# Eight transfers of each image issued from ScalarE's queue instead of SP's, with a lag margin in the planner

## The chip, the core and the metric

The kernel runs on one core of a Trainium2 chip. A core has five engines that run beside each other, each through its own list of instructions in order: TensorE (PE, matrix products), VectorE (DVE), ScalarE (ACT), GpSimd (POOL) and SyncE (SP), which in this kernel only issues DMA transfers. The metric is the device time of one execution in microseconds (us), the median of several runs.

## The reference

The input is x of shape (32, 96, 56, 56). Two layers follow. Each adds its result to x and begins with g, which is x normalised to mean 0 and variance 1 over groups of three channels with their planes (`gn`, with 1e-5 added to the variance); the kernel takes the statistics in `group_stats`.

Layer 0 is an inverted bottleneck with 4-bit weights and activations and a residual:

```python
g = gn(x)
h = act_q(bn(conv1x1(g, quant_w(w1)), ...))      # 96 -> 576
h = act_q(bn(depthwise3x3(h, quant_w(w2)), ...)) # 576, one 3x3 filter per channel
x = x + (g + bn(conv1x1(h, quant_w(w3)), ...))   # 576 -> 96
```

Layer 1 splits the channels of g = gn(x) into three parts of 32 (x_0, x_05, x_1) and adds a convolution of their results to x:

```python
x_0  = group_conv3x3(x_0, conv0_w * gate)                         # spatial part
Fre  = frft2d(x_05, alpha); Mix = group_conv1x1([Fre.real, Fre.imag], ...)
x_05 = abs(frft2d(Mix, -alpha)) / (H * W)                         # fractional part
x_1  = irfft2(group_conv1x1(rfft2(x_1) as real and imaginary))    # Fourier part
x    = x + conv3x3(concat(x_0, x_05, x_1), conv2_w) + conv2_b
```

alpha, the order of the fractional Fourier transform, comes for each image from a small network on the means of its own channels.

## The kernel before, in words

Images are handled one after another, but three streams are interleaved: the head of layer 0 (load, statistics, split), its body, and layer 1 of an earlier image. While layer 1 of image i runs, the body of layer 0 of image i+1 fills the gaps. Here and below the short names are those of the tiles in the profile.

*Layer 0.* `load` (L474) brings x. `split` (L704 to L710) normalises it and writes it as a high part hi (ScalarE) and the remainder lo (GpSimd). `expand` (L717) multiplies by w1 into the PSUM tile pe, in blocks b of 128 channels and four pixel parities u; ScalarE turns pe into 4-bit levels q1s (L662) and VectorE makes them integers (L666). `leave` and `enter` (L738, L746) bring q1s through DRAM (sd) into the layout d in which `depthwise` (L756) can run on TensorE, into pd. The same follows with q2s, gd and q (L777, L780), and `project` (L786) multiplies q by w3 into pp, which VectorE adds to x (L796). Names such as pe_0_3 and pd_0 are block and parity, and the group counted through.

*Layer 1.* After the statistics (L643, L651) `norm` (L863) writes the normalised middle 32 channels into rows 64 to 95 of F. `leave_x` stores them to DRAM (xd, L868), and `enter_x` loads them in two halves with image rows on the partitions (xh, L875). `forward_h` (pf, L975), `forward_w` (pu, L986), `inverse_w` (pi, L1002) and `inverse_h` (pv, L1013) are the transforms; their result pq is stored to DRAM (`leave_pq`: pd, L1024) and loaded back into F with channels on the partitions, in four transfers (`enter_pq`: L1029 twice and L1033 twice). `mix_f` (pz, L1047) multiplies F by the gated weights; squares, a square root and copies to the tile cat follow (L1054 to L1060). The spatial part writes ps (L1126) and the Fourier part pt, pr and px (L1069 to L1112); ScalarE and VectorE copy them to cat too (L1140, L1118, L1120). From cat VectorE forms the Winograd tiles V (L1158 to L1167) and TensorE the final convolution pc (L1179). `hidden`, `gate_row` and `gates` (ph, pg, pa, po) make the gates and alpha's table tab; outer (L907) and tab (L964) are ScalarE's part of it. The DRAM tile pd of the fractional part and the PSUM tile pd of the depthwise share a name.

*Buffers.* pe, pd (PSUM) and pp share two pairs of PSUM banks ("pair"); ps, px, pz, pc and the others of layer 1 share four single banks ("bank"). A matmul that takes a buffer again waits until the engine that reads it is through.

*The order.* `arrange` first writes the steps of the streams in a program order by estimated costs. Then `Order` computes the dependencies of all instructions, models a duration and a lag for each (`model`), packs them by list scheduling forward and backward in several trials (`pack`, `schedule`), and fixes the best trial's order on every engine (`hold`). So each engine's order is decided when the program is built. For a DMA the lag is the time from issue to data: 1.6 us, the time for its bytes, and 0.3 more for some. `moved` in `pack` is a running end of all transfers issued so far: one total for the whole core, so that in the plan a transfer stands behind all earlier ones.

Before the change every transfer of the main part is issued on SP, in one list. An SP instruction that waits (for VectorE, for an earlier transfer) holds all behind it. ScalarE issues only the constants at the start.

Of the kernel before, what the change touches and what calls it, by code (L numbers as in the profile page):

```python
# [63 lines left out]
C, H, W = 96, 56, 56  # L64
# [10 lines left out]
G = 32  # L75
# [3 lines left out]
BN_EPS = 1e-5  # L79
WINDOW, CHANGE = 3.4133, 0.09  # L80
TURNS, NEAR = 8, (2.0, 4.0, 8.0)
SLACK = 0.3


# [58 lines left out]
class Order:  # L143
# [64 lines left out]
    def model(self):  # L208


        self.took, self.lag, self.port, self.move, self.kind, self.work = [], [], [], [], [], []
        for i, e, access in zip(self.ins, self.eng, self.access):
            outs, ins = [a for a, w in access if w], [a for a, w in access if not w]
            n = max([_count(a) for a, _ in access], default=1)
            psum = [self.tiles.get(a.tensor.name, "")[:2] == "ps" for a in ins]
            wide = [a for a in ins if _count(a) > 1]
            lag = {"PE": 0.2, "Pool": 0.08}.get(e, 0.04)
            port, move, kind, work = False, 0.0, None, 0.0
            if i.opcode == "DMACopy":
                took = 0.47 if e == "SP" else 0.4  # L220
                for a in (outs[0], ins[0]):
                    run = size = _bytes(a.dtype)
                    dims, n = list(a.ap), 1.0
                    if self.tiles.get(a.tensor.name, "dram") != "dram":
                        n = dims.pop(0)[1]
                        move = max(move, _count(a) * size / 7000.0 * min(n / 16.0, 1.0))
                    for _, c in dims:
                        n *= c
                    for step, c in reversed(dims):
                        if step * size == run or c == 1:  # L230
                            run *= c
                        else:
                            break
                    run = min(run, n * size / 16)
                    move = max(move, math.ceil(n * size / run / 16) * (0.011 + run / 21e3))
                lag = 1.6 + move + (0.3 if ins[0].tensor.name.startswith(("in_x", "sd", "gd")) else 0.0)
            elif e == "PE":
                cols, weights, rows = _count(ins[0]), _count(ins[1]), ins[0].ap[0][1]
                full = all(str(a.dtype) == "dt.float32" for a in ins)
                beside = weights in (G, 64) and cols >= HN  # L240
                if i.is_transpose:
                    took = max(cols / 1175.0, 0.055)
                    work = cols / 1200.0
                elif full:
                    took = 2 * max(cols / 1175.0, min(weights * 0.85e-3, 1.0), 0.05)
                    work = cols / 600.0
                else:
                    took = max(cols / (2180.0 if "float32r" in str(ins[1].dtype) else 2350.0), 0.05)
                    work = cols / 2400.0
                if beside and not i.is_transpose:  # L250
                    took, work = took * weights / 128.0, work * weights / 128.0
                kind = (0 if rows <= 32 else 1 if rows <= 64 else 2), weights if beside else 0
                work *= rows / 128.0
            elif e == "Activation":
                out = _count(outs[0])
                bias = sum(_count(a) == 1 for a in ins) > 1
                took = 0.1 + bias * 0.1 + out / 960.0 + (0.08 if out > 700 and psum[0] else 0.13 if out < 8 else 0.0)
            elif e == "DVE":
                port = n > 8 and not any(psum)
                if port and i.opcode == "TensorScalarPtr" and len(wide) == 1:  # L260
                    took = 0.15 + n / 1920.0 + (0.12 if n >= 700 else 0.0)
                else:
                    port = port and len(wide) > 1
                    took = (0.14 if n > 8 else 0.16) + n / 960.0 + (0.06 if any(psum) and "ScalarPtr" in i.opcode else 0.0)
            elif e == "Pool":
                port = True
                took = 0.1 + n * (2.25 if len(wide) > 1 else 1.1) / 1000.0 if n > 8 else 0.5
            else:
                took = 0.1
            self.took.append(took)  # L270
            self.lag.append(lag)
            self.port.append(port)
            self.move.append(move)
            self.kind.append(kind)
            self.work.append(work)

    def pack(self, before, rank, near=0.0, back=False):
# [3 lines left out]
        n = len(self.ins)  # L281
# [4 lines left out]
        engines = sorted(set(self.eng))  # L286
        free, held = dict.fromkeys(engines, 0.0), dict.fromkeys(("DVE", "Pool"), 0.0)
        soon, now = {e: [] for e in engines}, {e: [] for e in engines}
        start, end, kind, moved = [0.0] * n, [0.0] * n, None, 0.0
        window, much, fast = 0, 0.0, False  # L290
        for k in range(n):
            if not lacks[k]:
# [1 line left out]
        for _ in range(n):  # L294
            t, e = min((free[e] if now[e] else max(free[e], soon[e][0][0]), e) for e in engines if now[e] or soon[e])
            while soon[e] and soon[e][0][0] <= t:
                k = heapq.heappop(soon[e])[1]
                heapq.heappush(now[e], (rank[k], k))
            k = now[e][0][1]
            if e == "PE" and near and self.kind[k] != kind:  # L300
                k = min([x for x in now[e] if self.kind[x[1]] == kind and x[0] < rank[k] + near], default=now[e][0])[1]
            if k == now[e][0][1]:
                heapq.heappop(now[e])
            else:
                now[e].remove((rank[k], k))
                heapq.heapify(now[e])
            if self.port[k]:
                t = max(t, held["Pool" if e == "DVE" else "DVE"])
            took = self.took[k]
            start[k], end[k] = t, t + took  # L310
            if e == "PE" and not back:
                took += CHANGE if kind != self.kind[k] else 0.0
                kind = self.kind[k]
                x, left = t, took
                while left > 1e-9:
                    while x >= (window + 1) * WINDOW - 1e-9:
                        window, fast, much = window + 1, much > 0.365 * WINDOW, 0.0
                    pace = 1.0 if fast else 0.5
                    part = min(left, ((window + 1) * WINDOW - x) * pace)
                    much += self.work[k] * part / took  # L320
                    left, x = left - part, x + part / pace
                end[k] = x
            free[e] = end[k]
            if self.port[k]:
                held[e] = end[k]
            lag = self.lag[k]
            if self.move[k] and not back:
                moved = max(moved, end[k] + 0.63) + self.move[k]
                lag = moved + self.lag[k] - self.move[k] - 0.63 - end[k]
            for q in then[k]:  # L330
                first = q if back else k
                alike = self.eng[q] == e and self.ins[first].opcode != "DMACopy"
                ready[q] = max(ready[q], end[k] + (0.0 if alike else self.lag[q] if back else lag))
                lacks[q] -= 1
                if not lacks[q]:
                    heapq.heappush(soon[self.eng[q]], (ready[q], q))
# [111 lines left out]
def block_kernel(ctx: ExitStack, tc: tile.TileContext, out: bass.AP, a: dict):  # L448
    nc = tc.nc
# [404 lines left out]
    def layer1(i):  # L854
# [10 lines left out]
            )  # L865
        def leave_x():
            s["xd"] = dp.tile([G, HW], F32, tag="xd", name=f"xd{i}")
            nc.sync.dma_start(out=s["xd"], in_=s["F"][2 * G : 3 * G])  # L868

        def enter_x():  # L870

            s["xh"] = p1.tile([2 * H, G // 2, W], F32, tag="h", name=f"xh{i}")
            for q in range(2):
                src = s["xd"][G // 2 * q : G // 2 * (q + 1)].rearrange("c (h w) -> h c w", w=W)
                nc.sync.dma_start(out=s["xh"][H * q : H * (q + 1)], in_=src)  # L875

        def norm1():

# [142 lines left out]

        def leave_pq():
            s["pd"] = dp.tile([2 * H, G + 1, W], F32, tag="pd", name=f"pd{i}")
            nc.sync.dma_start(out=s["pd"], in_=s["pq"])  # L1024

        def enter_pq():
            for q in range(2):
                src = s["pd"][H * q : H * (q + 1)]
                nc.sync.dma_start(  # L1029
                    out=s["F"][G * q : G * (q + 1)].rearrange("c (h w) -> c h w", w=W),  # L1030
                    in_=src[:, :G, :].rearrange("h c w -> c h w"),
                )
                nc.sync.dma_start(  # L1033
                    out=s["F"][3 * G + q : 3 * G + q + 1].rearrange("c (h w) -> c h w", w=W),
                    in_=src[:, G : G + 1, :].rearrange("h c w -> c h w"),
                )
# [483 lines left out]
```

## Time and profile before

| | |
|---|---|
| median of three runs | 3358.4 us (3348.12 to 3361.56) |
| the profiled execution | 3364.8 us, of which its span on the core 3363.0 us |
| mean granted TensorE clock | 0.949 |
| DMA | 469.92 MB, 140 GB/s over the span |
| SP's ring of queues (q1) | 432384 packets, 51.6% of 16 engines' span |
| ScalarE's ring of queues (q10) | 4184 packets, 0.3% |

The profile is of one execution and its times are to be set against 3364.8 us. For each group of instructions it gives the line, the engine, what is written from what, how many there were, and the idle time of the engine just before them with what ended it. A float32 matmul counts twice, since it runs as two passes. The durations of DMA issues are the time the issuing engine was held, not that of the data. Of the transfers concerned the trace shows the following on SP, by their instructions' durations (lowest, median, highest):

| transfer | line | issues | us |
|---|---|---|---|
| xd<-F | L868 | 32 | 0.308, 0.320, 0.326 |
| xh<-xd | L875 | 64 | 0.395, 0.935, 1.778 |
| pd<-pq | L1024 | 32 | 0.319, 0.322, 0.416 |
| F<-pd, 32 rows | L1029 | 64 | 0.315, 0.658, 1.002 |
| F<-pd, 1 row | L1033 | 64 | 0.730, 1.984, 3.050 |

### The profile page before, as it was taken

What the parts mean: (1) busy time and instruction counts of PE and PEld (TensorE: products, weight loads), DVE (VectorE), ACT (ScalarE), POOL (GpSimd) and SP (SyncE); (2) the same over time, 40 slices, a digit from 0 to 9 for tenths busy, and PEclk for the clock granted to TensorE, in tenths of its full rate; (3) what the DMA queues carried; (4) which work ended last, traced back from release to release, by engine and by line L of the source; (5) the groups of instructions that cost most, each with busy time, mean ns of one, the idle gap of its engine ahead of it and who ended that gap; (6) DMA issues with size and microseconds to landing.
All of it is one profiled execution on the core that took longest, in us unless ns stands there. A gap on an engine that the chain in (4) does not pass through costs nothing. (4 is left out here: it accounts for less than half of the span.)

```text
span 3363.0 us, 47042 instructions
## 1 busy us (share of the span) xinstructions
PE 2961.3 (88%) x17024; PEld 1824.1 (54%) x17024; DVE 2331.5 (69%) x4497; ACT 2085.9 (62%) x2792; POOL 585.2 (17%) x657
## 2 busy tenths in 40 slices
PE   3789998889998889999899999898998898999987
PEld 2455565455565555555455565455565455565544
DVE  5357677677777676777677777676777676777755
ACT  3566665576666566656566666566666576666543
POOL 3122101222101222111222011222111222101100
PEclk9898999999999999999999999999999999999987
DMA  4545564455655455654455655455655455655432
GB/s 125 150 118 143 147 166 133 116 144 144 167 159 141 117 145 137 168 141 134 124 146 151 173 146 149 121 146 138 168 157 142 116 145 143 166 162 148 115 89 51
DMA packets 436800, 469.92 MB, mean 140 GB/s; under 512 B 203174, under 2 KB 351640, under 8 KB 435544
## 3 DMA queue, kind: packets, MB, share of 16 engines
q1 hardware_dynamic: 432384, 464.18, 51.6%
q10 hardware_dynamic: 4184, 2.74, 0.3%
q8 instruction: 135, 2.21, 0.3%
q14 instruction: 97, 0.79, 0.1%
HBM read 266.85 MB, written 199.97 MB: 139 GB/s over the span
## 5 line engine op out<-in xcount | busy, mean ns | idle before, releaser
L662 ACT ACTIVATE q2s<-pd,o,s 128x784 uint8<-128x784 f32 x576 | 558.3, 1002 | 473.9 <-PE pd L756 454.5
L1179 PE MATMUL pc<-V,wcw 96*96 96x392 f32 x2304 | 834.9, 502 | 18.1 <-DVE V L1164 18.1
L662 ACT ACTIVATE q1s<-pe,o,s 128x784 uint8<-128x784 f32 (+1 forms) x640 | 624.1, 1004 | 219.7 <-PE pe L717 213.5
L717 PE MATMUL pe<-hi,w1r 96*128 96x392 f32 x1280 | 532.7, 416 | 68.0 <-ACT q1s L662 32.1
L1179 PEld LDWEIGHTS pc<-V,wcw 96*96 96x96 f32 x2304 | 366.9, 164 | 338.9 <-issue 319.7
L756 PE MATMUL pd<-d,dw 128*64 128x392 fp8e4 x4608 | 471.1, 345 | 85.1 <-DMA d<-sd 78.2
L717 PE MATMUL pe<-lo,w1r 96*128 96x392 f32 x1280 | 440.6, 344 | 3.2 <-POOL lo L708 3.2
L756 PEld LDWEIGHTS <-dw 128*64 128x64 bf16 x4608 | 243.3, 113 | 297.8 <-DMA d<-sd 104.8
L717 PEld LDWEIGHTS pe<-hi,w1r 96*128 96x128 f32 x1280 | 242.9, 190 | 181.4 <-ACT q1s L662 88.2
L708 POOL TENSOR_TENSOR lo<-v,hi 96x784 fp32r<-96x784 f32 x128 | 243.4, 1901 | 287.9 <-ACT hi L707 274.6
L1047 PE MATMUL pz<-F,g 98*32 98x392 f32 x1024 | 178.0, 700 | 129.3 <-DMA F<-pd 79.3
L786 PE MATMUL pp<-q,w3q 128*96 128x392 fp8e4 x1280 | 269.5, 359 | 12.1 <-DMA q<-gd 9.5
L717 PEld LDWEIGHTS pe<-lo,w1r 96*128 96x128 f32 x1280 | 244.2, 191 | 27.5 <-POOL lo L708 4.2
L786 PEld LDWEIGHTS <-w3q 128*96 128x96 fp8e4 x1280 | 167.2, 135 | 154.4 <-issue 70.6
L666 DVE TENSOR_SCALAR q2s<-q2s 128x392 uint32<-128x392 uint32 x288 | 119.4, 421 | 182.9 <-ACT q2s L662 180.0
L796 DVE SCALAR_TENSOR_TENSOR x<-pp,s,x 96x392 f32<-96x392 f32 x256 | 146.1, 617 | 103.9 <-PE pp L786 103.7
L654 POOL TENSOR_TENSOR stb<-veb,mhalf 96x1 f32<-96x1 f32 x32 | 17.9, 561 | 1143.8 <-DVE veb L653 1143.8
L1060 POOL COPY cat<-sq 32x392 f32<-32x392 f32 x256 | 157.8, 616 | 295.7 <-ACT sq L1056 286.1
L666 DVE TENSOR_SCALAR q1s<-q1s 128x436 uint32<-128x436 uint32 (+1 forms) x320 | 122.6, 389 | 120.5 <-ACT q1s L662 99.6
L704 DVE TENSOR_SCALAR v<-x,sta 96x784 f32<-96x784 f32 x128 | 87.0, 680 | 161.1 <-POOL lo L708 139.5
L1126 PE MATMUL ps<-s,g 128*128 128x392 f32 x512 | 193.6, 503 | 0.0
L1140 ACT ACTIVATE cat<-ps,b 32x392 f32<-32x392 f32 x256 | 158.8, 620 | 46.2 <-PE ps L1126 42.5
(156 smaller groups left out, 4267.8 us busy)
## 6 DMA issues: line engine op xcount, KB each, us to landing
d<-sd SPq DMA_DIRECT2D x288, 435.5 KB
gd<-q2s SPq DMA_DIRECT2D x288, 196.0 KB
sd<-q1s SPq DMA_DIRECT2D x256, 218.0 KB
q<-gd SPq DMA_DIRECT2D x128, 392.0 KB
x<-in_x_dram SPq DMA_DIRECT2D x128, 294.0 KB
out_dram<-x SPq DMA_DIRECT2D x128, 294.0 KB
pd<-pq SPq DMA_DIRECT2D x32, 808.5 KB
F<-pd SPq DMA_DIRECT2D x64, 392.0 KB
```

Source lines behind the costliest of these rows:

```text
L662: nc.scalar.activation(dst, ps, AF.Relu, bias=offset, scale=scale)
L666: nc.vector.tensor_scalar(w, w, 4, 0x0F0F0F0F, ALU.logical_shift_right, ALU.bitwise_and)
L708: nc.gpsimd.tensor_tensor(s["lo"][:, u, :], v, s["hi"][:, u, :].bitcast(F32), ALU.subtract)
L717: nc.tensor.matmul(ps[:, half, :HN], w1[:, 128 * b : 128 * (b + 1)], part[:, u, HN * half : HN * (half + 1)], start=(n == 0), stop=(n == 1),)
L756: nc.tensor.matmul(ps[64 * t : 64 * (t + 1), half, :HN], dw[n][:, 2 * t + y, :], view(s["d"][b, g][:, t, :], PQ * (14 * half + y), [[PQ, 1 ...
L786: nc.tensor.matmul(ps[:C, half, :HN], w3[:, b * C : (b + 1) * C], q2[b][:, u, HN * half : HN * (half + 1)], start=(b == 0), stop=(b == NB ...
L796: nc.vector.scalar_tensor_tensor(part, src, A3, part, ALU.mult, ALU.add)
L1047: nc.tensor.matmul(ps[G * j : G * (j + 1), :HN], s["g1"][: 3 * G + 2, G * q : G * (q + 1)], s["F"][:, 2 * HN * j + HN * h : 2 * HN * j + H ...
L1060: nc.gpsimd.tensor_copy(cat[G : 2 * G, r : r + 7, 1 : 1 + W], src)
L1126: nc.tensor.matmul(ps[:, :HN], s["g0"][:, 128 * t : 128 * (t + 1)], view(s0, PQ * (14 * half + t // 2) + t % 2, [[PQ, 14], [1, HH]]), star ...
L1140: nc.scalar.activation(dst, src, AF.Identity, bias=b0[2 * G : C], scale=1.0)
L1179: nc.tensor.matmul(ps[:C, :HN], wc[:, k, C * dx : C * (dx + 1)], V[:, :, dx : dx + W], start=(dx == 0), stop=(dx == 2),)
```

## The change

The eight transfers of the fractional part in each image (xd, the two of xh, pd, the four of F) are issued from ScalarE. In the planner each DMA's lag is 0.2 us longer (`MARGIN`), and `moved` becomes one running end for each issuing engine. Since the planner fixes the whole order, the order on all five engines is another one. In the lines of the changed kernel everything after the constant stands one line lower.

```diff
+MARGIN = 0.2
 SLACK = 0.3
...
-                lag = 1.6 + move + (0.3 if ins[0].tensor.name.startswith(("in_x", "sd", "gd")) else 0.0)
+                lag = 1.6 + MARGIN + move + (0.3 if ins[0].tensor.name.startswith(("in_x", "sd", "gd")) else 0.0)
...
-        start, end, kind, moved = [0.0] * n, [0.0] * n, None, 0.0
+        start, end, kind, moved = [0.0] * n, [0.0] * n, None, {}
...
             if self.move[k] and not back:
-                moved = max(moved, end[k] + 0.63) + self.move[k]
-                lag = moved + self.lag[k] - self.move[k] - 0.63 - end[k]
+                moved[e] = max(moved.get(e, 0.0), end[k] + 0.63) + self.move[k]
+                lag = moved[e] + self.lag[k] - self.move[k] - 0.63 - end[k]
...
         def leave_x():
             s["xd"] = dp.tile([G, HW], F32, tag="xd", name=f"xd{i}")
-            nc.sync.dma_start(out=s["xd"], in_=s["F"][2 * G : 3 * G])
+            nc.scalar.dma_start(out=s["xd"], in_=s["F"][2 * G : 3 * G])
...
-                nc.sync.dma_start(out=s["xh"][H * q : H * (q + 1)], in_=src)
+                nc.scalar.dma_start(out=s["xh"][H * q : H * (q + 1)], in_=src)
...
-            nc.sync.dma_start(out=s["pd"], in_=s["pq"])
+            nc.scalar.dma_start(out=s["pd"], in_=s["pq"])
...
-                nc.sync.dma_start(
+                nc.scalar.dma_start(
                     out=s["F"][G * q : G * (q + 1)].rearrange("c (h w) -> c h w", w=W),
                     in_=src[:, :G, :].rearrange("h c w -> c h w"),
                 )
-                nc.sync.dma_start(
+                nc.scalar.dma_start(
                     out=s["F"][3 * G + q : 3 * G + q + 1].rearrange("c (h w) -> c h w", w=W),
                     in_=src[:, G : G + 1, :].rearrange("h c w -> c h w"),
                 )
```

In the order of the built program, on ScalarE in an image of the middle part, pd's issue stands after the last q2s and the last v of pv's inputs; then hi, two cats of ps_0, the first F, hi, the second F, the two of L1034, and then the other six cats of ps. xd's issue stands between q2s of pd_9 and of pd_10; xh's two between outer and q1s of pe_4_1. On TensorE ps, all but three of the forty pp, the start of px and pe_0_0 stand between the last pv and the first pz (before: ps, eight pp, px and the last two depthwise groups), and pd_0 follows pe_1_3 and pz_1_1.

## The prediction

> **What bounds the kernel now.** I read the page's busy table, then TensorE's waits, then the timelines of TensorE and of SP's queue at the longest wait. The table names the bound:
>
> ```profile
> PE 2961.3 (88%) x17024; PEld 1824.1 (54%) x17024; DVE 2331.5 (69%) x4497; ACT 2085.9 (62%) x2792; POOL 585.2 (17%) x657
> ```
>
> TensorE idles 402 of 3363 us, about 9 us of each image. Its waits (total us, times, longest):
>
> ```profile
> PE pz L1047 <- DMA F<-pd: 79.3, 18, 6.0
> PE pd L756 <- DMA d<-sd: 78.2, 43, 6.0
> PE pz L1047 <- ACT cat L1120: 44.1, 10, 4.7
> PE pe L717 <- ACT q1s L662: 32.1, 93, 1.8
> PE pf L975 <- DMA xh<-xd: 15.3, 25, 1.6
> ```
>
> The ten waits put down to cat sit at the same place and are as long (4.0 to 4.7 us) as the eighteen for F, so I count 28 waits, 123 us, at the first pz. SP's queue, then TensorE, of one such image:
>
> ```profile
> 1518.05 0.32 SPq L1024 DMA_DIRECT2D pd<-pq  x1
> 1518.48 0.37 SPq L780 DMA_DIRECT2D q<-gd  x1
> 1523.74 1.18 SPq L1029 DMA_DIRECT2D F<-pd  x2
> 1524.97 2.11 SPq L1033 DMA_DIRECT2D F<-pd  x1
> 1527.13 0.53 SPq L777 DMA_DIRECT2D gd<-q2s  x1
> 1527.70 0.78 SPq L1033 DMA_DIRECT2D F<-pd  x1
> ```
> ```profile
> 1531.81 5.40 PE L1047 MATMUL pz<-F,g 98*32 98x392 f32 x26 [4.83 <-DMA F<-pd]
> 1537.14 2.19 PE L786 MATMUL pp<-q,w3q 128*96 128x392 fp8e4 x12
> ```
>
> From pd's issue it is 5.7 us to the first F issue and 13.8 to pz; TensorE was ready at 9.0. The projections (pp) that could have covered this stand behind pz. Note gd's issue caught between two F issues.
>
> The d waits matter as much for what follows. In eight of the 27 images from 2 to 28 the first depthwise group (pd_0), or the pc that stands there, waits about 4 us as well; these take 105.4 us from one end of pv to the next, the other nineteen 98.8. From the end of pv in image 2 (395.87, by TensorE's timeline) to that in image 29 (3116.89) it is 2721.0 / 27 = 100.8 an image.
>
> **What the skill says.** "DMA: Bandwidth & Descriptors", section "Issuing engines are not separate DMA queues": SP's and ScalarE's DMAs run on the same 16 engines, and issuing from both saves only sequencer time. So I expect no bandwidth; the page's 140 GB/s shows that none is short. The same page, "Queues, rings and completion order": each of the two owns a ring per engine, served in turn by packets. No run here shows that; a transfer then no longer stands behind SP's. "Perfetto Trace Analysis", "DMA Instruction — HWDGE (DVE, Sync)": the profiled duration is the sequencer's hold, not the movement. The trace agrees: F issues last 0.3 to 3.1 us while the data land 8 us after the first. "TensorE: Matmul & The Clock Gate", Part 1: after an idle window of about 3.4 us the array runs at half clock. The trace agrees: 16 pd matmuls take 2.83 us after a 4.0 us wait and 1.52 elsewhere.
>
> **The change, part by part.**
>
> *Removed from SP.* Eight issues an image (xd, two xh, pd, four F) and the waits before them. SP is no bottleneck; what frees is gd and q behind F: the gd issued at 1527.13 was ready some 4 us earlier (its q2s left ScalarE at 1522.2). The new order uses this: 37 of 40 pp stand between pv and pz.
>
> *Added to ScalarE.* By SP's medians: xd 0.32, xh 2 x 0.94, pd 0.32, F 1.18 + 2.11 + 0.78 = 4.1; sum 6.6 us an image, 211 us in all, ScalarE at 2297 (68%). Lower bound 2.6 us (eight at 0.32), upper 6.6 plus about 3 us standing for pd to land; I take 6.6. A part lies in idle time: ScalarE waits 454 us for pd and 214 for pe. Behind an F issue stand the cats of ps_0, which free the bank for px_1, then q1s of pe_0: two cats, then F, hi, F, F, F, then the third and fourth. The fourth ends 3.9 us later than without issues; about 1 us of it reaches TensorE (0 to 3).
>
> *The margin and the separate running totals.* 0.2 us per transfer and the `moved` split change only the plan; they cost nothing themselves, but the whole order moves. What the new order is worth needs a template. Image 1 of the kernel before has nearly the new order (36 pp before pz, pz among the pe, pd_0 right after pe_1_3):
>
> ```profile
> 321.42 0.44 PE L717 MATMUL pe<-hi,w1r 96*128 96x392 f32 x1 [1.76 <-ACT q1s L662]
> 328.11 2.82 PE L756 MATMUL pd<-d,dw 128*64 128x392 fp8e4 x16 [2.36 <-DMA d<-sd]
> 331.46 4.90 PE L1179 MATMUL pc<-V,wcw 96*96 96x392 f32 x8 [0.52 <-DVE V L1164]
> ```
> ```profile
> 295.87:395.87 100.00, 92.51 (x515) 55.73 (x514) 71.77 (x138) 62.91 (x85) 18.35 (x20) 0.93 0.52 140
> 395.87:492.93 97.06, 89.21 (x535) 55.57 (x534) 72.45 (x139) 64.95 (x87) 17.32 (x20) 0.98 0.56 150
> ```
>
> (Columns: stretch, us, busy PE, PEld, DVE, ACT, POOL, TensorE clock, DMA share, GB/s.) No wait at pz, yet it took 100.0 us and its clock was 0.93, against 97.1 and 0.98 for the next image. It also lacks pd_16, pd_17 (1.5 us) and four pp (0.7), which image 2 does later: with them 102.2.
>
> *Why pd_0 waits now.* In the image of 1616 to 1722, ScalarE ended pe_0_3 at 1647.66, VectorE 1648.08, d's issue came at 1651.87 and pd_0 began at 1655.93: 8.3 us. In the new order, from the end of pe_0_3 on ScalarE, TensorE needs the table load 1.28, square root 0.53, cat 0.46 and pe_1_1 1.0, then pe_1_3 0.7: ready after 4.0. So pd_0 waits 8.3 - 4.0 = 4 us in every image, since pc cannot fill: its cat comes from pz. Before, eight pc stood there in ordinary images.
>
> *Differences from the template.* F issues on ScalarE +1.0. The square root now follows pe_0_3, not precedes it: the 1.76 wait goes, 1.1 of which pd_0's wait takes back, so -0.7. V later by the same ScalarE delay, +0.8 (0 to 2). pd_12 moved behind pf loses its d wait (0.74), -0.7. pd_15 then waits for a bank behind a table load and tab, +1.0 (0 to 1.6). xd goes out some 2 us earlier after pvb, because VectorE writes F before the torus, but xh's issue waits for outer and then holds ScalarE 1.9 us from pe_4_1: 0 (-1 to +1). Lower-cost issue on ScalarE's own ring, and gd and q free of F: -1.4 (-3 to 0), an estimate from the 2.4 to 2.9 us that the two L1033 issues take on SP's. Sum 0.0.
>
> So 102.2 an image against 100.8: +1.4 x 28 = +39 us. Start and tail keep their shape: in the last image pv to pz holds the same ps and px, so 0.
>
> Profiled execution: 3364.8 (span 3363.0 and 1.8 around it). It lies 6.4 above the median of 3358.4. Forecast 3364.8 + 39 - 6.4 = 3397 us.
>
> **The rivals.**
>
> *The pz wait is won.* Place: pd_0. If SP, freed, brings d there at most 2 us late, the long images go too: 27 x (100.8 - 98.8) = 54, and ordinary ones keep a little of pz's 4.4, say 0.5 x 19 = 10: 3358 - 64 = 3294. For it: 123 us of real waits, more work before pz (in image 1 it starts 15.1 us after pv, where ordinary images were ready after 10.1), and warm pz (16 in 1.52 us in image 1, 26 in 5.40 above). Against it: the chain of 8.3 us has no F in it. It decides from a pd_0 wait below 2 us.
>
> *Exchange.* Wait and half clock move from pz to pd_0 at equal price: within 17 us, 3358.
>
> *ScalarE becomes the pace.* Issues hold it longer than SP, or F's issue stands for pd; each us beyond slack reaches TensorE through the pair of banks. At +3 us more an image: 3397 + 84 = 3481. Against: it is busy only 65 of 100 us.
>
> That the change doesn't do what it says is excluded: in the built order the eight issues stand on ScalarE.
>
> **How the numbers follow.** Template case 0.50, ScalarE's pace 0.07, won 0.28, exchange 0.15. With 0.5% (17 us) as the bound: faster 0.28, same 0.15, slower 0.57. The template's own range is 3376 to 3440 (the bounds above, partly cancelling). For 8 in 10 I go from 3290, the won case, to 3450.
>
> **What would show it.** Right: F<-pd no longer leads TensorE's waits; d<-sd exceeds 100 us, about 4 us at pd_0 in most images; pd_0 at half clock; ScalarE about 70%; period near 102. Wrong: pd_0 starting within 2 us of pe_1_3, or the wait at pz still there because F's issue came late on ScalarE; the first makes it faster, the second slower still.

## The result, and the profile after

| | before | changed |
|---|---|---|
| median, us | 3357.2 (3348.1 to 3361.6, 4 runs) | 3514.9 (3496.5 to 3532.7, 4 runs) |
| ratio, 95% interval | | 1.0473 (1.0414 to 1.0532) |
| profiled execution, span | 3364.8, 3363.0 | 3532.65, 3530.9 |
| mean granted TensorE clock | 0.949 | 0.921 |
| end of pv to end of pv, images 2 to 29 | 100.8 | 106.5 |

The change costs 158 us, where 39 were forecast. Of the 168 us between the two profiled spans, 154 lie in the 27 images from 2 to 29 (27 x 5.7).

The busy table of the changed kernel, and TensorE's waits (total us, times, longest):

```profile
PE 3077.7 (87%) x17024; PEld 1879.0 (53%) x17024; DVE 2319.5 (66%) x4497; ACT 2078.7 (59%) x2792; POOL 617.8 (17%) x657
```
```profile
PE pd L757 <- DMA d<-sd: 120.9, 43, 5.7
PE pe L718 <- ACT q1s L663: 85.3, 82, 2.4
PE pf L976 <- DMA xh<-xd: 40.6, 22, 3.4
PE pd L757 <- ACT q2s L663: 37.2, 59, 1.3
PE pp L787 <- DMA q<-gd: 30.0, 13, 4.8
...
PE pz L1048 <- DMA F<-pd: 8.1, 2, 6.2
```

The 123 us of waits at pz are gone. The wait for d has come in their place, and beside it several smaller ones have grown to about three times what they were before, or more: q1s 85.3 (32.1), xh 40.6 (15.3), q2s 37.2 (5.2). Two places of one image on TensorE's timeline:

```profile
1499.02 0.45 PE L718 MATMUL pe<-hi,w1r 96*128 96x392 f32 x1 [1.60 <-ACT q1s L663]
...
1504.18 2.82 PE L757 MATMUL pd<-d,dw 128*64 128x392 fp8e4 x16 [4.19 <-DMA d<-sd]
1507.43 2.93 PE L1180 MATMUL pc<-V,wcw 96*96 96x392 f32 x4 [0.42 <-DVE V L1165]
...
1557.96 0.42 PE L976 MATMUL pf<-e2t,xh 112*112 112x114 f32 x2 [1.63 <-DMA xh<-xd]
```

And the same two places by stretch (columns as in the prediction: stretch, us, busy PE, PEld, DVE, ACT, POOL, clock, DMA share, GB/s):

```profile
1499.00:1504.00 5.00, 0.97 (x4) 0.65 (x4) 2.39 (x6) 3.12 (x5) 2.61 (x6) 0.74 0.50 134
1504.00:1508.00 4.00, 3.40 (x17) 1.64 (x18) 3.56 (x5) 1.95 (x2) 1.73 (x1) 0.50 0.54 167
1508.00:1512.00 4.00, 4.00 (x18) 1.57 (x18) 3.88 (x5) 0.23 (x2) 0.00 (x0) 0.55 0.51 162
```
```profile
1556.00:1558.00 2.00, 0.37 (x4) 0.22 (x3) 1.67 (x4) 1.55 (x4) 0.35 (x2) 1.00 1.02 312
1558.00:1562.00 4.00, 4.00 (x28) 3.27 (x30) 3.75 (x9) 1.50 (x3) 0.00 (x0) 0.68 0.80 213
```

After each of the two waits TensorE is busy almost without a break, but at half clock for most of the time. I read such windows 1 us wide over images 2 to 28 and split each stretch of an image into *work* (busy time times granted clock), *slow* (the rest of the busy time, what the low clock adds) and *idle*. Mean us of an image, length = work + slow + idle:

| stretch | before | changed |
|---|---|---|
| end of pv to pz | 14.5 = 10.2 + 0.1 + 4.2 | 16.0 = 15.2 + 0.2 + 0.6 |
| pz to the first pc | 21.3 = 15.9 + 2.9 + 2.5 | 21.6 = 12.8 + 2.4 + 6.4 |
| pc to pvb | 34.0 = 33.6 + 0.3 + 0.1 | 33.3 = 32.3 + 0.9 + 0.1 |
| pvb to pf | 16.7 = 16.0 + 0.0 + 0.8 | 16.8 = 13.3 + 0.8 + 2.6 |
| pf to the end of the next pv | 14.3 = 12.2 + 0.1 + 2.0 | 18.8 = 15.7 + 1.8 + 1.3 |
| image | 100.8 = 87.8 + 3.5 + 9.5 | 106.5 = 89.3 + 6.1 + 11.1 |

(Rounded one by one, so sums can be off by 0.1.) The projections now fill the stretch before pz, and its idle time falls from 4.2 to 0.6. But 5.0 us of work were put where 3.6 us of idle time went, so the stretch itself is longer. The two stretches up to pc, which a chain of layer 1 runs through (pd, F, pz, square root, cat, V), became not shorter but 1.9 us longer together. From pvb to pf, where another chain runs (F, xd, xh), 2.7 us less work is placed and the length stays; the last stretch then holds 3.5 us more work and is 4.5 longer. The 1.5 us more of *work* are not due to the coarseness of the windows: cut where the granted clock itself changes, the two traces give the same 87.8 and 89.3. They may be the more frequent change between kinds of matmuls; that was not tried.

### The profile page after: what moved, and what is told of

Its sections match the earlier page's. It is cut to its first block, busy times and chain, and to the rows that moved or that the text cites. A ratio compares the mean times of both kernels' runs of the same rounds, so it can differ in the third digit from the quotient of the medians.

```text
span 3530.9 us, 46921 instructions
## 1 busy us (share of the span) xinstructions
PE 3077.7 (87%) x17024; PEld 1879.0 (53%) x17024; DVE 2319.5 (66%) x4497; ACT 2078.7 (59%) x2792; POOL 617.8 (17%) x657
## 5 line engine op out<-in xcount | busy, mean ns | idle before, releaser
L1180 PE MATMUL pc<-V,wcw 96*96 96x392 f32 x2304 | 851.3, 509 | 19.3 <-DVE V L1165 19.3
L757 PE MATMUL pd<-d,dw 128*64 128x392 fp8e4 x4608 | 525.5, 372 | 161.9 <-DMA d<-sd 120.9
L718 PE MATMUL pe<-hi,w1r 96*128 96x392 f32 x1280 | 532.1, 419 | 116.5 <-ACT q1s L663 85.3
L757 PEld LDWEIGHTS <-dw 128*64 128x64 bf16 x4608 | 267.9, 121 | 439.0 <-issue 162.3
L718 PE MATMUL pe<-lo,w1r 96*128 96x392 f32 x1280 | 455.9, 359 | 3.8 <-POOL lo L709 3.7
L718 PEld LDWEIGHTS pe<-lo,w1r 96*128 96x128 f32 x1280 | 250.1, 196 | 29.1 <-POOL lo L709 7.5
L667 DVE TENSOR_SCALAR q1s<-q1s 128x436 uint32<-128x436 uint32 (+1 forms) x320 | 151.0, 476 | 164.1 <-ACT q1s L663 161.0
L1061 POOL COPY cat<-sq 32x392 f32<-32x392 f32 x256 | 191.3, 747 | 317.0 <-ACT sq L1057 308.5
L1141 ACT ACTIVATE cat<-ps,b 32x392 f32<-32x392 f32 x256 | 158.0, 618 | 142.8 <-issue 73.4
L787 PEld LDWEIGHTS <-w3q 128*96 128x96 fp8e4 x1280 | 153.8, 127 | 137.0 <-issue 65.6
L667 DVE TENSOR_SCALAR q2s<-q2s 128x392 uint32<-128x392 uint32 x288 | 103.1, 358 | 127.4 <-ACT q2s L663 126.4
L708 ACT CAST hi<-v 96x784 fp32r<-96x784 f32 x128 | 107.9, 843 | 132.1 <-DVE v L705 119.6
L1210 DVE TENSOR_TENSOR md<-mc,pc 96x392 f32<-96x392 f32 x128 | 71.4, 558 | 141.1 <-ACT q1s L663 69.9
```

Of the source, the lines that this page charges most:

```text
L667: nc.vector.tensor_scalar(w, w, 4, 0x0F0F0F0F, ALU.logical_shift_right, ALU.bitwise_and)
L708: nc.scalar.copy(s["hi"][:, u, :], v)
L718: nc.tensor.matmul(ps[:, half, :HN], w1[:, 128 * b : 128 * (b + 1)], part[:, u, HN * half : HN * (half + 1)], start=(n == 0), stop=(n == 1),)
L757: nc.tensor.matmul(ps[64 * t : 64 * (t + 1), half, :HN], dw[n][:, 2 * t + y, :], view(s["d"][b, g][:, t, :], PQ * (14 * half + y), [[PQ, 1 ...
L787: nc.tensor.matmul(ps[:C, half, :HN], w3[:, b * C : (b + 1) * C], q2[b][:, u, HN * half : HN * (half + 1)], start=(b == 0), stop=(b == NB ...
L1061: nc.gpsimd.tensor_copy(cat[G : 2 * G, r : r + 7, 1 : 1 + W], src)
```

## The experiments

The change mixes two things: another order on all engines, and another engine for eight issues. In the first two runs the planner is told one thing and the transfers do the other. All medians below stand against the kernel before in the same batch (3355 to 3360 us).

**newplan_sp**: the changed kernel's plan, the issues on SP.

Against the changed kernel, cut to what matters (the first lines are for the plan only, and the last two stand for all eight issues):

```diff
+        self.eng = [
+            "Activation" if i.opcode == "DMACopy" and any(a.tensor.name.startswith(("xd", "pd")) for a, _ in acc) else e
...
-            nc.scalar.dma_start(out=s["xd"], in_=s["F"][2 * G : 3 * G])
+            nc.sync.dma_start(out=s["xd"], in_=s["F"][2 * G : 3 * G])
```

> The order of the changed kernel on TensorE, VectorE, GpSimd and of all other work of ScalarE is kept instruction by instruction; only the eight transfers are issued from SP, at the places that the same plan gives them. Theory A (the new order costs the time, the issuing engine hardly matters): 3515 us within 20, d still waited for at pd_0 in nearly every image, mean clock 0.92. Theory B (ScalarE's issues and its standing for pd and xd cost the time): 3360 to 3400 us, clock back near 0.95.

**oldplan_act**: the mirror image; the plan of before, the eight issues on ScalarE.

> The reverse: the order of the kernel before on all engines, with the eight transfers put into ScalarE's list at the times that the old plan gave them on SP. Theory A: 3357 us within 20. Theory B: 3450 us or more, with waits of TensorE for ScalarE's q1s and q2s behind the issues. A smaller share for the queue, 10 to 50 us, would be the hold of 4 to 7 us an image on ScalarE showing through in part.

| order \ issued on | SP | ScalarE |
|---|---|---|
| of before | 3358 | 3440.8, ratio 1.0248 (1.0224 to 1.0273) |
| of the change | 3486.6, ratio 1.0389 (1.0360 to 1.0418) | 3514.9 |

Each theory holds in part, and neither number came out. The order alone costs about 127 us; the queue costs 81 us in the old order and some 28 in the new one (the two intervals leave 6 to 50). With the new order on SP the waits for d and q1s are nearly those of the changed kernel, and that for xh is longer (67.6 against 40.6):

```profile
PE pd L761 <- DMA d<-sd: 120.6, 46, 5.3
PE pe L722 <- ACT q1s L667: 74.3, 66, 2.4
PE pf L980 <- DMA xh<-xd: 67.6, 29, 4.8
```

**margin_only** (all on SP, `lag = 1.6 + 0.2 + move`) and **queue_only** (ScalarE, no margin, one running total):

> All transfers on SP as before, only the margin of 0.2 us in the planner's lags. Theory A: the margin draws a new order, whose time is not tied to the queue at all: anything from 3340 to 3500 us, and the pz wait or the pd_0 wait as it falls. Theory B: 3357 us within 17, since nothing moves to ScalarE.

> The eight transfers on ScalarE, without the margin and with one running total for the core. Theory A: a third order, 3340 to 3550 us, neither that of before nor that of the change. Theory B: 3480 to 3530 us, since ScalarE carries the same issues as in the changed kernel. A third theory, that the separate running totals let the planner believe in a transfer that stands behind no other and so draw pz and pd_0 too early, expects 3360 to 3400 here.

margin_only: 3321.3 us, ratio 0.9884 (0.9857 to 0.9912): the order that the margin alone draws is the faster one. Its order leaves a wait of about 1 us at pz and puts pd_0 13.5 us behind the first pc; slow time is 1.5 us an image. queue_only: 3495.5, ratio 1.0394 (1.0344 to 1.0443). margin_only lies below what either theory expected; queue_only lies in the ranges of both A and B and does not decide between them. The loss comes with moving the issues; the margin and the separate totals aren't needed for it.

**before_trial9**: why do plans with the queue moved lose even when SP issues? Their orders have one shape: 36 to 40 pp before pz in nearly every image (8 before), and pd_0 ahead of the first pc. Among the 24 orders that the search of the kernel *before* had found there is one of that shape.

```diff
-        self.end, _, self.at = min(trials)
+        self.end, _, self.at = trials[9]
```

> The kernel before with nothing changed in its planner's model and all transfers on SP; only another of the 24 orders that the same search found is held (the tenth of them). It has the shape of the changed kernel: 36 of 40 pp before pz, pd_0 before the first pc. Theory D (this shape of the order costs the time, whatever draws it and whatever queue issues): 3460 to 3500 us, as the new order on SP (3487), with a wait of about 4 us for d at pd_0. Rival (the loss belongs to details of the one order that the change drew): within 60 us of 3358.

3457.8 us, ratio 1.0298 (1.0274 to 1.0321), 2 us below the expected range. TensorE's first waits there:

```profile
PE pd L756 <- DMA d<-sd: 140.1, 65, 5.6
PE pe L717 <- ACT q1s L662: 69.9, 66, 1.9
```

An order of this shape, drawn by the old model and issued on the old queue, thus costs 100 us, most of the 127. It is one order, and it differs from that of before in more than the shape; the rest was not traced.

**Which wait of the shape costs?** The half clock was the first suspect. Five matmuls on constants were put ahead of pz in the old order, or ahead of pd_0 in the new one, into the tile that the real matmuls then overwrite; the planner doesn't see them.

In the diff, for pz, `fill` issues so many matmuls `matmul(ps, mw2[:, :128], mw2[:, :HN])`:

```diff
+                if h == q == 0:
+                    fill(ps[:, :HN], 5)
```

> The kernel before with its order untouched on every engine; five more float32 matmuls of 128x392 (about 3.4 us of TensorE) on constants are put ahead of the first pz of each image, into the tile that pz then overwrites. Theory C (much of what a wait of 4 us costs is the half clock that it brings on for the next 3.4 to 6.8 us): the low clock at pz disappears, TensorE's busy time without the fill falls by about 3 us an image, total 3260 to 3290 us although work was added. Rival (the clock falls for another reason, such as the kind of work, and a filled wait is worth nothing): 3360 within 17, or later where the fill overruns F.

> The changed kernel with its order untouched; the same five matmuls ahead of pd_0 of each image, into the tile that pd_0 then overwrites. Theory C: of 16 us at half clock in an image some 7 to 10 stand behind pd_0; they go, 3.5 to 5 us an image, total 3380 to 3425 us. If the wait at pd_0 alone carried the loss of the new order (my forecast's mechanism), the kernel would then stand within 40 us of the one before; if the stretch around pf carries a share as well, it stays above 3400. Rival: 3515 within 20.

> As after_filled, with three filling matmuls (3.0 us at the 0.5 us a pass seen there) in place of five, which overran d by over 1 us. If half clock behind pd_0 costs what the accounting says (some 3 us of 6.1 slow us an image stand between pz and the end of pc), of which the chain to V leaves about 1.5 us to be won: 3460 to 3490 us. If pc waits for V in any case, 3505 to 3520.

before_filled: 3327.8 us, ratio 0.9909 (0.9875 to 0.9942). The time at half clock fell from 8.5 to 2.9 us an image, and the total by 30 us, a third of what was expected. after_filled: 3517.7, ratio 1.0478 (1.0439 to 1.0517): nothing. With three matmuls (after_filled3) 3506.2, ratio 1.0444 (1.0423 to 1.0466): 9 us less, within the intervals. The timeline of after_filled:

```profile
1498.82 4.99 PE L467 MATMUL pd<-mw 128*128 128x392 f32 x10
1503.74 1.52 PE L775 MATMUL pd<-d,dw 128*64 128x392 fp8e4 x16
1506.22 1.56 PE L1198 MATMUL pc<-V,wcw 96*96 96x392 f32 x4 [0.97 <-DVE V L1183]
```

pd_0 runs at full clock (1.52 instead of 2.82), and pc then waits for V. Five matmuls are too long, though: d was issued at 1498.77, pd_0 starts 4.0 us after that issue on average in the changed kernel, and here it starts 5.0 us after it, so the fill costs about 1 us. The three of after_filled3 do not overrun, and there the first pc waits for V in 21 of the 27 images, 0.8 us on average (changed kernel: 0.3). In most images, then, pc starts when the chain over the square root and cat is through, not when TensorE is. In the changed kernel the last square root ends 30.8 us after pd's issue on average (before: 29.0); pz itself is spread from 15.1 to 27.4 us (13.3 to 23.7). A fill takes away the half clock behind a wait and leaves the wait: what an earlier d would win was not tried.

**after_pf_later**: one depthwise group moved, on TensorE alone, to fill the wait at pf. The text below counts 16 matmuls (1.5 us) for a group; a group is 8, and in the trace the edit has moved 8 of the 48 behind pf, 0.8 us.

> The changed kernel; on TensorE alone, in 30 of the images, the next depthwise group (16 matmuls, 1.5 us) is taken from just behind pf to just ahead of it. All other engines keep their order. Theory E (TensorE comes to pf too early, since the plan thinks xh lands sooner than it does, and the wait of 1.5 us and the half clock behind it are lost time): 1.5 to 3 us an image, 3430 to 3475 us, with the wait for xh below 0.5 us an image. Rival (the chain from xh over u to pv sets the end of the stage, and pf starts as late as before): 3500 to 3530.

3498.9 us, ratio 1.0439 (1.0397 to 1.0481). In the trace the wait for xh falls from 40.6 to 23.9 us, that for q2s rises:

```profile
PE pd L793 <- ACT q2s L699: 51.3, 72, 1.7
...
PE pf L1012 <- DMA xh<-xd: 23.9, 21, 2.7
```

The gain of 16 us is inside the intervals. The 40 us or more of theory E did not come, but half as much was moved as it assumed, and part of the wait for xh is left: the theory is weakened, not excluded.

**What the queue costs.** In the old order the eight issues were split: only xd and xh on ScalarE (oldplan_x_act), or only pd and F (oldplan_pd_act).

> The order of before, with only xd and the two xh issued from ScalarE at the old plan's times; pd and F stay on SP. The whole move cost 81 us in this order. If each transfer costs by the time that ScalarE is held (3 of the 8 issues, 2.2 of 6.6 us): 25 to 30 us. If the loss comes from F's data landing about 1 us later at pz: 5 to 15 us here.

> The complement: pd and the four F from ScalarE, xd and xh on SP, in the order of before. By ScalarE's hold: 50 to 55 us. By F's later landing at pz (14.2 instead of 13.3 us after pd's issue, with the longer half clock that follows): 65 to 80 us, with the wait at pz at 5.5 us or more.

oldplan_x_act: ratio 1.0042 (1.0028 to 1.0055), 14 us. oldplan_pd_act: 3423.8, ratio 1.0184 (1.0149 to 1.0219), 66 us. Together they make up the 81 of oldplan_act. In oldplan_pd_act F's last issue ends as before (10.25 us after pd's), yet pz starts 1.0 us later, and pc 2.1 us later. Two causes were possible: a q load that SP no longer holds back runs beside F (it is issued between F's first and last issue in 26 of the 27 images from 2 to 28, in none of them in the kernel before); or ScalarE, held by the issues, is late with its copies. ScalarE's timeline of one such image, and below it that of an image before:

```profile
1537.86 2.50 ACTq L1037 DMA_DIRECT2D F<-pd  x1
1540.41 0.59 ACT L1144 ACTIVATE cat<-ps,b 32x392 f32<-32x392 f32 x1 [2.83 <-issue]
1540.46 0.73 ACTq L1037 DMA_DIRECT2D F<-pd  x1
1541.01 0.62 ACT L1144 ACTIVATE cat<-ps,b 32x392 f32<-32x392 f32 x1
1541.66 0.84 ACT L711 CAST hi<-v 96x784 fp32r<-96x784 f32 x1
1542.53 2.50 ACT L1144 ACTIVATE cat<-ps,b 32x392 f32<-32x392 f32 x4
1545.05 0.85 ACT L1124 COPY cat<-px 32x392 f32<-32x392 f32 x2
```
```profile
1522.68 2.53 ACT L1140 ACTIVATE cat<-ps,b 32x392 f32<-32x392 f32 x4 [0.47 <-PE ps L1126]
1525.23 0.84 ACT L707 CAST hi<-v 96x784 fp32r<-96x784 f32 x1
1526.10 2.52 ACT L1140 ACTIVATE cat<-ps,b 32x392 f32<-32x392 f32 x4
1528.64 0.85 ACT L1120 COPY cat<-px 32x392 f32<-32x392 f32 x2
```

**oldplan_pd_qlate** takes the q load away from F, **oldplan_rows_sp** takes the two one-row F issues (L1037 above, 2.50 and 0.73 us) back to SP. Cut from the diffs (in the first, q are the loads of q under way with F, f the four transfers of F; the second is against oldplan_pd_act):

```diff
+            for k in q[:1]:
+                tc.add_manual_dep(self.ins[k], self.ins[f[-1]].name, wait, reason="behind F")
```
```diff
-                nc.scalar.dma_start(
+                nc.sync.dma_start(
                     out=s["F"][3 * G + q : 3 * G + q + 1]...
```

> As oldplan_pd_act (order of before, pd and F from ScalarE: 3424 us), but the load of q that SP issues while F is under way waits until F's last transfer has landed; nothing else is moved. Theory G (F lands 1.0 us later because a q load now runs beside it on the same 16 DMA engines, which SP's list had kept behind F): from F's last issue to pz 3.1 us again instead of 4.1, total 3355 to 3385 us. Rival (ScalarE's ring or ScalarE's own hold makes F late): pz as late as before this edit, 3410 to 3435 us, or later where pp then waits for q.

> As oldplan_pd_act (3424 us), but the two one-row F transfers go back to SP; pd and the two 32-row F stay on ScalarE, still in the order of before. The one-row issues held ScalarE some 3.3 of the 4.6 us an image that F held it there, with the cats of ps and px behind them. Theory H (ScalarE's hold makes the cats late, so the banks of pz, the square root and V, and pc starts 2.1 us later): the last cat of ps ends within 1.5 us of the kernel before, total 3360 to 3385 us. Rival (pd's or F's data on ScalarE's ring land late, whatever ScalarE does): 3410 to 3430 us.

oldplan_pd_qlate: 3427.2, ratio 1.0202 (1.0179 to 1.0226). Theory G was right on the transfer and wrong on the time: from F's last issue to pz it is 3.2 us again (4.1), and nothing is won, since pc still comes 36.9 us after pd's issue (before 34.6). oldplan_rows_sp: 3353.9, ratio 0.9986 (0.9970 to 1.0002): all of the 66 us are back. Means over images 2 to 28, us from pd's issue:

| | F holds ScalarE | last cat of ps | pz starts | last square root | first pc |
|---|---|---|---|---|---|
| before | 0 | 11.1 | 13.3 | 29.0 | 34.6 |
| oldplan_pd_act | 4.6 | 14.6 | 14.3 | 31.2 | 36.7 |
| oldplan_pd_qlate | 4.7 | 14.7 | 13.5 | 31.4 | 36.9 |
| oldplan_rows_sp | 1.2 | 12.1 | 12.8 | 29.1 | 34.6 |

The square root and pc follow the cats and not the start of pz: with pz early again and the cats late (oldplan_pd_qlate) pc stays late, with the cats 2.5 us earlier it is back. A last cat 1.1 us later than before costs nothing in oldplan_rows_sp, where pz starts 0.5 us earlier.

**calibrated_sp, calibrated_act, calibrated_filled**: the planner gets the durations of the trace, first with all on SP (and the margin of 0.2), then with the issues on ScalarE (margin 0.3), then the first of these with two filling matmuls ahead of pz.

```diff
+                if name[1].startswith("xh"):
+                    took, lag = 0.93, lag + 1.5
+                elif name[0].startswith("pd"):
+                    took = 2.0 if outs[0].ap[0][1] == 1 else 0.6
+                elif name[1].startswith(("pd", "sd")):
+                    lag += 0.9
```

> All transfers on SP, the margin of 0.2, and the planner's figures of the transfers concerned set to what the trace of before shows: SP held 2.0 us by a one-row F and 0.6 us by a 32-row F, 0.93 us by xh, lags 1.5 us longer for xh and 0.9 us for pd and sd. It draws an order in which pz follows pv directly and pd_0 stands far behind the first pc. If waits that the plan knows of are covered: 3290 to 3330 us, at or below the order with the margin alone (3321). If the draw decides more than the figures: 3330 to 3420.

> The changed kernel (eight transfers on ScalarE, separate totals) with the same measured figures in the planner as in calibrated_sp and a margin of 0.3. The plan again puts all 40 pp before pz and pd_0 before pc. Theory D (the shape decides): 3400 to 3480 us, 100 or more above calibrated_sp. If measured figures are all that the planner lacked: 3300 to 3340 us.

> calibrated_sp (3303 us) with two filling matmuls, 2.0 us of TensorE, ahead of pz, where 2.5 us of wait and 3.4 us at half clock an image are left. Theory C: the slow time at pz (1.6 us an image) goes for the most part, 3255 to 3280 us. If pz or V is set by ScalarE's cats and not by TensorE's clock: 3290 to 3310 us.

calibrated_sp: 3303.3 us, ratio 0.9837 (0.9809 to 0.9866), faster than both kernels; in its order, as in that of margin_only, pd_0 stands far behind the first pc. calibrated_act: 3609.5, ratio 1.0760 (1.0714 to 1.0806), 130 us worse than the top of what was expected; all pp stand before pz, and of 108.1 us an image 14.1 are idle. Measured figures in the planner do not rescue the move. calibrated_filled: 3300.6, ratio 0.9823 (0.9799 to 0.9848), the same as without the fill: at pz the half clock is no longer what the end depends on. What is left in calibrated_sp:

```profile
PE pz L1054 <- DMA F<-pd: 86.2, 31, 5.7
PE pd L763 <- ACT q2s L669: 38.8, 66, 2.0
```

It still waits for F, with more of the kernel's other waits covered.

The profiled executions also tell what the orders of this shape have in common. From the end of pv to the first pc the changed kernel, newplan_sp, queue_only, before_trial9 and calibrated_act take 37.6, 37.1, 38.8, 38.2 and 38.1 us an image, against 35.8 before and 34.6 and 33.9 in the two faster orders, margin_only and calibrated_sp. From there to the next end of pv they take 68.9, 67.9, 65.5, 65.9 and 70.0, against 65.0. So 1.4 to 3.0 us are lost up to pc in all five; the larger loss behind pc, in the changed kernel's plan, is not common to the shape.

## Why the prediction was wrong

The direction and most of the local signs were right; the size was not, and the time lies beyond the range (3290 to 3450). The direction owes something to luck: the seven differences from the template cancelled to 0.0, and slower had been given 0.57.

- *"F<-pd no longer leads"*, *"d<-sd exceeds 100 us, about 4 us at pd_0"*, *"pd_0 at half clock"*: right. 8.1 us instead of 123, 120.9 us, 4.19 us in the image shown (3.3 us on average), 2.82 us for 16 matmuls.
- *The chain of 8.3 us that makes pd_0 wait*: the wait is there. But taking away the half clock behind it won 9 us, inside the intervals, since the chain to V ends only about 2 us later. The half clock at pd_0 is thus not the price of the order; what the wait itself costs was not tried.
- *"Image 1 ... with them 102.2"* and the differences from it: this is the step that failed. Without the terms of ScalarE's issues and queue (+1.0, the +0.8 for V, -1.4) the sum asks for 101.8 us with the issues on SP; newplan_sp has 105.0. Of the 3.2 us between them 2.2 lie behind pf and 1.4 up to pvb, less 0.4 won from pvb to pf. Two terms that had been booked as gains were none.
  - *"pd_12 moved behind pf loses its d wait (0.74), -0.7"*. From pf to the end of pv the forecast comes to 13.9 + 2.2 - 0.7 + 1.0 = 16.4 us; newplan_sp takes 18.6. In image 1 that stretch holds 16 depthwise matmuls, in the changed kernel 48 in nearly every image. In image 1 the wait of 0.74 is that of pd_14, which stands behind pf already; pd_12 and pd_13 stand ahead of pf there. Moving them took 16 matmuls from a stretch that did not get shorter for it: xh sets when it ends. The table of stretches shows the price: 2.7 us of work out of pvb to pf with no shortening, and 1.8 us of low clock behind pf, for which I had taken 0.
  - *"The 1.76 wait goes ... so -0.7"*. It stayed: in all 27 images of the changed kernel TensorE waits for q1s for 1.4 to 2.4 us between pz and pc (1.60 in the image shown), and so it does in newplan_sp; before, 0.4 to 0.6. Up to pvb newplan_sp takes 70.2 us, image 1 69.5, and the forecast 68.8.
- *"F issues on ScalarE +1.0"* and *"about 1 us of it reaches TensorE (0 to 3)"*: the mechanism was the right one, shown by oldplan_rows_sp; but in the old order 66 us, 66 / 28 = 2.4 us an image, reach it, near the upper end of the bounds.
- *"Lower-cost issue on ScalarE's own ring, and gd and q free of F: -1.4"*: no such gain. In oldplan_pd_act the freed q load delays F by about 0.8 us, and keeping it back again wins nothing either. With +1.0 and the +0.8 for V this made the queue +0.4 us an image; measured are some 28 us, +1.0 an image, in the new order. And that no bandwidth is short is true of the mean of 140 GB/s only. In the 4 us before pz in the prediction's image the DMA engines were busy for 0.84 of the time, in the 4 us before the next pf for 0.97 (next to last column):

```profile
1527.80:1531.80 4.00, 0.00 (x0) 0.02 (x1) 2.61 (x5) 3.37 (x7) 1.55 (x2) 0.80 0.84 116
1597.70:1601.70 4.00, 3.35 (x33) 2.55 (x32) 2.67 (x7) 3.88 (x7) 0.35 (x2) 1.00 0.97 205
```

So another queue would hardly bring F or xh sooner there. oldplan_rows_sp fits that, where F's last issue ends 2.7 us earlier and pz starts 0.5 us earlier.

- *"xd ... 0 (-1 to +1)"*: 14 us, 0.5 an image in the old order, inside the bounds.
- *"ScalarE about 70%"*: a mistake of accounting. The page doesn't count issues as busy, so ScalarE stands at 59%. The issues held it 5.6 us an image (6.6 forecast); with them it is 64%. They appear only as idle time, 73.4 us of it before the cats of ps, put down to "issue".

The rival in which ScalarE becomes the pace (3481) names a real part of the loss, but not the larger one.

That the new order and not the queue costs the larger part is shown (newplan_sp, oldplan_act). That it is the shape is likely: every order of the shape that was run lost 100 us or more, before_trial9 with the old model and queue too, and the shape came with the move in every plan tried (the change, queue_only, calibrated_act). That in the changed kernel the loss is the work placed into the wrong stretch is read from the table and not shown: two direct attempts on single waits won 9 and 16 us, both unclear. In before_trial9 pd_12 and pd_13 stand ahead of pf, and only 1.1 us an image is lost behind pf, but 2.6 between pz and pc and 2.1 between pvb and pf. Why the planner prefers this shape once ScalarE issues wasn't tried.

## What to carry to other kernels

Before a transfer is moved to a computing engine, ask what stands behind its issue there: an issue can hold its engine for microseconds, and copies queued behind it can free the buffers that the critical engine takes next. Where a planner fixes the order, separate the plan from the edit (old plan with the new queue, new plan with the old queue) before explaining the sum. And a wait that goes wins time only if no other chain sets the next step: compare the length of each stretch with the work that is placed in it, since work moved out of a stretch whose length a chain sets has to be paid for again elsewhere, as the table suggests here behind pf.

## What the runs showed of the hardware

The hold of an issue depends on what its own queue has before it. First oldplan_pd_act, with the one-row F issues on ScalarE behind the two 32-row ones; then oldplan_rows_sp, with the one-row ones on SP while the 32-row ones go through ScalarE (operation of the tile F by queue: durations in ns, lowest, median, highest):

```profile
L1033 ACTq DMA_DIRECT2D F<-pd x64: 316/597/1281, 193.0 to 3352.7; - x64
L1037 ACTq DMA_DIRECT2D F<-pd x64: 732/1466/3521, 194.2 to 3355.8; - x64
```
```profile
L1037 SPq DMA_DIRECT2D F<-pd x64: 734/805/1229, 194.7 to 3299.4; - x64
L1033 ACTq DMA_DIRECT2D F<-pd x64: 309/561/1302, 194.8 to 3298.9; - x64
```

A one-row issue takes at least 0.73 us; what lies above it, up to 2.8 us, shrinks to 0.5 at most when the large transfers are in the other queue. It is not a matter of the engine: on SP behind the 32-row ones, in the kernel before, the one-row issues took 1.98 us in the median and up to 3.05. With two queues pz starts 0.5 us earlier than before (12.8 against 13.3 us), which is what they are worth here. The Trainium skill says that issuing from several engines saves only the sequencer's time, and that this time is usually small beside the transfer ("DMA: Bandwidth & Descriptors", "Issuing engines are not separate DMA queues"). The first half agrees with these runs. The second doesn't hold here: in oldplan_pd_act the four F issues hold ScalarE for 4.6 of the 8.9 us from the first of them to pz, and with the two one-row issues back on SP 66 us of the kernel are gone.

Half clock came in pieces of 3.4 us: in the kernel before, the stretches of images 2 to 28 last 3.4 or 6.8 us; in the changed kernel most last 3.4, 6.8 or 10.2, the longest 17. Behind a wait the half clock can last longer than the wait: at pd_0 in the image shown, TensorE works on at half clock for 7.4 us after a wait of 4.19 (from 1504.2 to 1511.6, by the clock of the stretches above). But this time is lost only in part where another chain sets the next step: taken away, it was worth 30 us in before_filled and at most 9 in after_filled and after_filled3. Half clock also followed shorter waits: at pf in the image shown, after a wait of 1.63 us among light work (TensorE busy for 0.37 of 2.0 us), the clock is half for one piece of 3.4 us. The skill names an idle window of about 3.4 us ("TensorE: Matmul & The Clock Gate", Part 1); here no single wait had to last so long.
